# Linear attention and RWKV feed-forward on one core: a new order for the first tiles and the late weights

## The chip, the cores and the metric

The kernel runs on one core of a Trainium2 chip. The metric is the device time of one launch in microseconds (us). Engines are called TensorE (PE in the profile, with PEld for its weight loads), VectorE (DVE), ScalarE (ACT), GpSimd (POOL) and SyncE (SP, which issues most DMAs).

## The reference

The input `x` has 16 sequences of 1024 rows of 512 numbers, all in fp32. One layer is computed: linear attention with a residual and a layernorm, then an RWKV feed-forward with a residual and a layernorm.

```python
qkv = x @ Wqkv.T + bqkv
q, k, v = jnp.split(qkv, 3, axis=-1)
q = rmsnorm(q, gq); k = rmsnorm(k, gk)
q, k, v = split(q), split(k), split(v)            # 16 heads of 32
q = apply_rope(q, cos, sin); k = apply_rope(k, cos, sin)
qf = relu(q); kf = relu(k)
vpad = concatenate([v, ones])
vk = einsum('bhlp,bhld->bhpd', vpad, kf)          # per sequence and head
res = einsum('bhpd,bhld->bhlp', vk, qf)
attn = res[..., :-1] / (res[..., -1:] + 1e-6)
x = layernorm(x + rmsnorm(attn @ Wout.T + bout, gout))
# feed-forward: xr, xk mix each row with the row before it
r = sigmoid(xr @ W_r.T); k = square(relu(xk @ W_k.T))
x = layernorm(x + r * (k @ W_v.T))
```

## The kernel before

The 16384 rows are cut into 128 tiles of 128 rows. Phase A (the first half of the span) goes once over all tiles in slots, one tile `i` in each (`slot(i)`), eight tiles to a sequence. Phase B then makes the attention's output and the feed-forward in steps of 512 rows. This case is about the beginning of phase A.

A product of fp32 data is made as three products of float32r data: each operand is split into a high part (a cast on ScalarE) and a low part (the rest, a subtraction on VectorE or GpSimd), and high x high, high x low and low x high are summed in one PSUM bank. So q of a tile takes 12 matmuls of 128x128 by 128x512: four chunks of the 512 inputs times three (`proj(i, 0)`; `proj(i, 1)` is k). The bias comes in one of two ways: for tiles 0 and 1 by two more matmuls against a row that holds it (`row_h`, `row_l` with `sel_b`), for the later ones by a seed, a copy of the bias into the PSUM bank before the products (`seed`, in the profile a ScalarE COPY psq<-b_qk on line 157).

In a slot, TensorE makes q and k of tile `i` from the transposed input (`xt`, split by `split_x`), and adds the 12 products of the tile before into the keys' sum of the sequence, `pskx`, four banks (`add_kx(i - 1)`, from keys `kh`, `kl` and the untransposed input `xnh`, `xnl`). `rope` takes q and k from PSUM: the sum of squares (ScalarE, tile `junk`), two multiplications with tables and an addition (VectorE, tiles `t`, `ro`); q goes to DRAM (`q_d`); for the keys GpSimd makes the scale `rstd_all` and ScalarE the scaled, rectified `kh` and `ro`; GpSimd adds `ro` into `acc`.

The rotation needs four tables for each position in a sequence, two for q and two for k, with the gains `gqk` multiplied in. They are made once, for tiles 0 to 7 (`tables(i)`), and stored to DRAM (`tab_d`), from which the later tiles load them. The cosine table is a multiplication on GpSimd. The sine table, whose signs and places differ, is one matmul of `cs` and `gt` for each of q and k, which ScalarE copies out of PSUM; before, its bank is one of the `pskx` banks for tiles 0 and 1 (`psb`) and a bank of its own for tiles 2 to 7 (`pstab`). Each table has one SBUF buffer.

The q and k weights are loaded in eight blocks of 256 KB (`stage_qk`) and split (`split_qk`). Ten matmuls on zeros (`pswarm`) stand ahead of the first product. The 20 blocks of the other weights (v, out, and the three of the feed-forward) are late weights: from slot 5 on one block is loaded and split in each slot (`late_weight`, which calls `split_w`).

The order: an instruction stream is written down in Python and a scheduler with its own estimates orders each engine's stream, except where `in_order(engine)` holds the written order. Before, it holds for all five engines up to the end of the prologue (`start`), and for TensorE up to slot 7 (`start_pe`). Every engine works through its stream in order. DMAs take eight completion semaphores in turn, so that a DMA waits for the landing of the eighth before it.

The prologue before, in the written order of TensorE: warm-up, q of tile 0, `psb` products for `gt` and `cs`, q of tile 1, the sine tables of tile 0, k of tile 0, k of tile 1. Then slot by slot: (for tiles from 2) q, k, the key products of the tile before, the two sine tables of the next tile.

Of the kernel before, what the change touches and what calls it, by code (L numbers as in the profile page):

```python
# [24 lines left out]
NWARM = 10  # L25
# [8 lines left out]
def kernel(  # L34
# [259 lines left out]
    with ExitStack() as a_ctx:  # L294
# [44 lines left out]
        def split_w(hi, lo, src, low, dma, tag="xw", bufs=3):  # L339
            w = tp.tile([P, DIM], F32, tag=tag, bufs=bufs, name="wstage")  # L340
            dma.dma_start(out=w, in_=src)
            S.copy(hi, w)
            low.tensor_sub(lo, w, f32(hi))

        first = {}

        def seed(i):
            for j in range(2):
                first[i, j] = seeded(f"ps{'qk'[j]}{i}", b_qk[:, j * DIM : (j + 1) * DIM])
# [9 lines left out]
        def tables(i):  # L359

            t = i % 8
            if i < 8:
                tab_d[t] = dram.tile([P, 2, 2, DIM], F32, name=f"tab_d{t}")
            for j in range(2):
                for n in (1, 0):
                    tb = wa.tile([P, DIM], F32, tag=f"tab{j}{n}", name=f"tab{j}{n}{i}")
                    tab[i, j, n] = tb
                    if i >= 8:
                        nc.sync.dma_start(out=tb, in_=tab_d[t][:, j, n, :])
                        continue  # L370
                    g = g_qk[:, j * DIM : (j + 1) * DIM]
                    if n == 0:
                        c = angle[0][:, t, :].unsqueeze(1).to_broadcast([P, 2 * HEADS, HH])
                        G.tensor_mul(rows(tb), rows(g), c)
                    else:
                        ps = kx_bank(j) if i < 2 else bank(f"pstab{i}{j}")
                        T.matmul(ps, lhsT=cs[0:KT, t, :], rhs=gt[0:KT, j, :], start=True, stop=True)
                        S.copy(tb, ps)
                    nc.sync.dma_start(out=tab_d[t][:, j, n, :], in_=tb)
# [18 lines left out]

        mask = te.tile([P, P], BF16, name="mask")
        V.memset(mask, 0.0)  # L400
        for h in range(P // DH):
            V.memset(mask[h * DH : (h + 1) * DH, h * DH : (h + 1) * DH], 1.0)
        ones = te.tile([P, P], F32R, name="ones")
        V.memset(f32(ones), 1.0)
# [3 lines left out]
        def proj(i, j):  # L408

            seeds = i > 1  # L410
            ps = first.pop((i, j)) if seeds else bank(f"ps{'qk'[j]}{i}")
            cols = slice(j * DIM, (j + 1) * DIM)
            for c in range(NC_):
                for n, (a, b) in enumerate(((xh, "h"), (xh, "l"), (xl, "h"))):
                    T.matmul(  # L415
                        ps,
                        lhsT=a[i][:, c, :],
                        rhs=w_qk[b][:, c, cols],
                        start=(not seeds and c == 0 and n == 0),
                        stop=(seeds and c == NC_ - 1 and n == 2),  # L420
                        skip_group_check=True,
                    )
            if not seeds:
                for n, r in enumerate((row_h, row_l)):
                    T.matmul(
                        ps,
                        lhsT=sel_b[:, j, :],
                        rhs=r,
                        start=False,
                        stop=(n == 1),  # L430
                        skip_group_check=True,
                    )
            return ps

        acc, ros = {}, {}

        def rope(i, ps):

            ss = wa.tile([P, 2], F32, tag="ss", bufs=3, name=f"ss{i}")
            ro = []  # L440
            for j in range(2):
                S.activation(junk(f"{i}{j}"), ps[j], AF.Square, accum_out=ss[:, j : j + 1])
                r = wa.tile([P, DIM], F32, tag=f"ro{j}", bufs=1 + j, name=f"ro{j}{i}")
                t2 = wa.tile([P, DIM], F32, tag="t2", name=f"t2{j}{i}")
                V.tensor_mul(t2, ps[j], tab.pop((i, j, 1)))
                V.tensor_mul(ps[j], ps[j], tab.pop((i, j, 0)))
                V.tensor_add(halves(r), halves(ps[j]), halves(t2)[:, :, ::-1, :])
                ro.append(r)
                if j == 0:
                    q_d[i] = dram.tile([P, DIM], F32, name=f"q_d{i}")  # L450
                    nc.sync.dma_start(out=q_d[i], in_=r)
            V.tensor_scalar(ss, ss, 1.0 / DIM, RMS_EPS, ALU.mult, ALU.add)  # L452
            rsqrt(rstd_all[:, i, :], ss)
            k = ro[1]
            kh = tk.tile([P, DIM], F32R, tag="kh", bufs=2, name=f"kh{i}")
            kl = tk.tile([P, DIM], F32R, tag="kl", bufs=2, name=f"kl{i}")
            S.activation(kh, k, AF.Relu, scale=rstd_all[:, i, 1:2])
            S.activation(k, k, AF.Relu, scale=rstd_all[:, i, 1:2])  # L458
            V.tensor_sub(kl, k, f32(kh))
            b, t = divmod(i, 8)  # L460
            ros[i] = k
            if t == 1:
                acc[b] = tx.tile([P, DIM], F32, tag="acc", name=f"acc{b}")
                G.tensor_add(acc[b], ros[i - 1], k)
            if t > 1:
                G.tensor_add(acc[b], acc[b], k)  # L466
            return kh, kl
# [114 lines left out]
        def late_weight():  # L582
            n, w, c = late.pop(0)
            if n in "ao":
                to = {"a": w_a, "o": w_o}[n]
                split_w(to["h"][:, c, :], to["l"][:, c, :], w[:, c, :], V, nc.sync)
                return
            m = te.tile([P, 2, DIM], F32R, tag="m", bufs=2, name=f"w{n}{c}")
            split_w(m[:, 0, :], m[:, 1, :], w[:, c, :], V, nc.sync)
            nc.sync.dma_start(out=w_d[n][:, c, :, :], in_=f32(m))  # L590
# [7 lines left out]
        start_pe.enter_context(in_order(mybir.EngineType.PE))  # L598
        start = a_ctx.enter_context(ExitStack())
        for e in ("SP", "Activation", "DVE", "Pool"):  # L600
            start.enter_context(in_order(getattr(mybir.EngineType, e)))

        row = tp.tile([P, DIM], F32, tag="q", bufs=3, name="row")
        V.memset(row, 0.0)
        m0 = te.tile([P, 2, DIM], F32R, tag="m", bufs=2, name="m0")
        V.memset(f32(m0[:, 0, :]), 0.0)


        for n in range(NWARM):
            T.matmul(bank(f"pswarm{n}"), lhsT=m0[:, 0, 0:P], rhs=m0[:, 0, :], start=True, stop=True)  # L610
        stage = {}

        def stage_qk(j, c, dma=nc.sync):
            n = NC_ * j + c
            w = tp.tile([P, DIM], F32, name="wstage", **[dict(tag="x", bufs=NT), dict(tag="xw", bufs=3), dict(tag="q", bufs=3)][(n >= NT) + (n >= NT + 3)])
            dma.dma_start(out=w, in_=wqkv[:, c, j * DIM : (j + 1) * DIM])
            stage[j, c] = w

        def split_qk(j, c, low=V):
# [4 lines left out]
            low.tensor_sub(l, w, f32(h))  # L624

        load_xt(0)
        for c in range(NC_):
            stage_qk(0, c, (nc.sync, nc.scalar)[c % 2])
# [5 lines left out]

        S.copy(table, mhalf)
        angle = [tp.tile([P, 8, HH], F32, tag="y", bufs=2, name=f"angle{n}") for n in range(2)]
        nc.sync.dma_start(out=angle[1], in_=sin_t)
        stage_qk(1, 0)
        load_xt(1)
        for c in range(1, NC_):  # L640
            stage_qk(1, c)
        load_xn(0)
        nc.sync.dma_start(out=angle[0], in_=cos_t)
        g_qk = wp.tile([P, 2 * DIM], F32, tag="m", bufs=NC_, name="g_qk")
        nc.sync.dma_start(out=g_qk, in_=gqk.partition_broadcast(P))
        b_qk = ca.tile([P, 2 * DIM], F32, name="b_qk")
# [20 lines left out]
        V.tensor_scalar(msk[:, 1, :], msk[:, 0, :], -1.0, None, ALU.mult)  # L667
        cs6 = wp.tile([P, 8, P], F32, tag="m", bufs=NC_, name="cs6")[:, :, 0:KT]
# [5 lines left out]
        split_qk(0, 0)  # L674
        split_qk(0, 1)
# [4 lines left out]
        split_qk(0, 2)  # L680
        split_qk(0, 3)
        ahead = {(0, 0): proj(0, 0)}
        split_x(1)
        split_qk(1, 0, G)
        split_qk(1, 1, G)
        gt = wp.tile([P, 2, DIM], F32R, tag="m", bufs=NC_, name="gt")
        for j in range(2):
# [8 lines left out]
            )  # L696
        cs = wp.tile([P, 8, P], F32R, tag="m", bufs=NC_, name="cs")
# [16 lines left out]
        split_qk(1, 2, G)  # L714
        split_qk(1, 3, G)
        ahead[1, 0] = proj(1, 0)
        tables(0)
        ahead[0, 1] = proj(0, 1)
        split_xn(0)
        ahead[1, 1] = proj(1, 1)  # L720
        start.close()

        def slot(i):
# [6 lines left out]
            qk = [ahead.pop((i, j)) if i < 2 else proj(i, j) for j in range(2)]  # L730
            if 0 < i < N - 1:
                split_x(i + 1)
            if i > 0:
                split_xn(i)
# [8 lines left out]
            if i >= 1:  # L743
                add_kx(i - 1)
            state[i] = rope(i, qk)
            if not last:
                tables(i + 1)
                if i > 0:
                    seed(i + 1)
            if i == 2:  # L750
                with tc.issue_after(load.ins):
                    constants()
            if i >= 5 and late:
                with tc.issue_after(load.ins):
                    late_weight()
# [26 lines left out]
        for i in range(N - 1):  # L782
            slot(i)
            if i == 7:
                start_pe.close()
# [281 lines left out]
```

## Time and profile before

| | |
|---|---|
| time, median of 4 runs | 2729.34 us (2726.69 to 2729.4) |
| profiled execution | 2729.34 us, span 2727.5 us |
| TensorE busy | 2694.1 us (99%) |
| VectorE, ScalarE, GpSimd busy | 2170.1 (80%), 1882.2 (69%), 700.9 (26%) us |
| DMA | 433.29 MB, mean 159 GB/s |

A timeline line gives the start in the span, the duration, the engine, the line of the program and the operation; in square brackets stands how long the engine was idle before it, and what ended that. A line of waits gives who waited, for what, the sum in us, how often, and the longest. A line of stretches gives from:to, length, the busy time with the number of instructions for each engine asked for, the granted clock of TensorE, the share of the DMA engines' time and GB/s. TensorE's durations overlap: in full flow a product of 512 columns starts each 0.227 us and is listed with 0.39 us. The granted clock is listed as 1.00 at the start of the span too, where the products step by 0.43 us.

### The profile page before, as it was taken

The page shows a single profiled execution, that of the slowest core. Times are in us where ns is not written, and L with a number is a line of the kernel's source. Part 1 is how long each engine was busy: PE and PEld are TensorE (multiplying, and loading weights), DVE is VectorE, ACT ScalarE, POOL GpSimd, SP SyncE. Part 2 cuts the span into 40 slices and gives each one's busy share as a digit, 9 for nine tenths or more (in the row PEclk, how much of TensorE's full clock was granted, in tenths as well). Part 3 has the DMA queues.
Part 4 walks back from the last instruction along what each step waited for, and adds up shares of the span by engine and source line. Part 5 has one row for each costly group of instructions (what it writes and reads, how often), then busy time and mean ns, then how long its engine had stood idle before and what let it go on. Part 6 is the DMA issues. An engine that isn't in the chain of part 4 may idle for free.

```text
span 2727.5 us, 40197 instructions
## 1 busy us (share of the span) xinstructions
PE 2694.1 (99%) x12558; PEld 2233.1 (82%) x12558; DVE 2170.1 (80%) x4880; ACT 1882.2 (69%) x3822; POOL 700.9 (26%) x800
## 2 busy tenths in 40 slices
PE   8999999999999999999999999999999999999998
PEld 6778888888888888887888888888888888888887
DVE  6888787887787788776888878888887878888874
ACT  5666666666666656657777787777777777777775
POOL 5222222222222222223322222222222222222221
PEclk9999999999999999999999999999999999999999
DMA  6699777766777877764332232323233233313210
GB/s 231 205 307 317 234 247 232 231 227 225 230 232 248 263 246 245 233 205 157 101 105 74 93 109 64 111 89 110 65 95 110 73 98 93 116 59 108 75 56 34
DMA packets 232015, 433.29 MB, mean 159 GB/s; under 512 B 24676, under 2 KB 24932, under 8 KB 231800
## 3 DMA queue, kind: packets, MB, share of 16 engines
q1 hardware_dynamic: 231504, 430.18, 48.8%
q8 instruction: 99, 1.62, 0.2%
q14 instruction: 116, 0.95, 0.1%
q10 hardware_dynamic: 296, 0.53, 0.1%
HBM read 314.19 MB, written 116.42 MB: 158 GB/s over the span
## 4 chain that ended last, share of the span: by engine, by line
PE 84%; DVE 2%; DMA 2%; ACT 1%; issue 1%; POOL 0%; SPq 0%; POOLq 0%; DVEq 0%; ACTq 0%
PE psr L178 13%; PE psk L178 13%; PE psv L178 13%; PE psy L178 13%; PE psq L415 9%; PE pskx L485 9%; PE psk L415 9%; PE psqt L163 2%; PE pst L163 2%; PE psm L570 1%; PE pskv L528 1%; DMA q<-q_d 0%; DMA tab<-tab_d 0%; DMA q_d<-ro 0%; PE pskv L536 0%
## 5 line engine op out<-in xcount | busy, mean ns | idle before, releaser
L178 PE MATMUL psk<-mkh,w_k 128*128 128x512 f32 x1024 | 333.8, 397 | 2.3 <-ACT mkh L831 2.3
L178 PE MATMUL psv<-w_v,kah 128*128 128x512 f32 x1024 | 321.9, 395 | 0.0
L178 PE MATMUL psy<-mb,qth 128*128 128x512 f32 x1024 | 319.9, 389 | 0.0
L178 PE MATMUL psr<-w_r,mrh 128*128 128x512 f32 x1024 | 317.8, 396 | 0.0
L466 POOL TENSOR_TENSOR acc<-acc,ro 128x512 f32<-128x512 f32 x96 | 159.0, 1656 | 273.2 <-ACT ro L458 230.4
L178 PEld LDWEIGHTS psk<-mkh,w_k 128*128 128x128 f32 x1024 | 192.0, 189 | 41.6 <-ACT mkh L831 2.7
L178 PEld LDWEIGHTS psy<-mb,qth 128*128 128x128 f32 x1024 | 192.2, 188 | 39.9
L178 PEld LDWEIGHTS psr<-w_r,mrh 128*128 128x128 f32 x1024 | 188.8, 188 | 36.9
L178 PEld LDWEIGHTS psv<-w_v,kah 128*128 128x128 f32 x1024 | 187.8, 188 | 36.2
L142 POOL TENSOR_TENSOR rstd_all<-ss,mhalf 128x2 f32<-128x2 f32 x128 | 93.0, 726 | 475.4 <-DVE ss L452 453.9
L833 POOL TENSOR_TENSOR mkl<-mixk,mkh 128x512 fp32r<-128x512 f32 x127 | 165.8, 1306 | 184.3 <-ACT mkh L831 183.4
L415 PE MATMUL psq<-wqk_h,xh 128*128 128x512 f32 x512 | 201.8, 394 | 5.8 <-ACT psq L157 4.9
L415 PE MATMUL psk<-wqk_h,xh 128*128 128x512 f32 x512 | 199.6, 390 | 3.0 <-ACT psk L157 3.0
L415 PE MATMUL psq<-wqk_l,xh 128*128 128x512 f32 x512 | 200.8, 392 | 0.6 <-DVE wqk_l L624 0.6
L178 PE MATMUL psk<-mkl,w_k 128*128 128x512 f32 x512 | 200.5, 392 | 0.2 <-DVE mkl L833 0.2
L415 PE MATMUL psq<-wqk_h,xl 128*128 128x512 f32 x512 | 200.5, 392 | 0.0
L178 PE MATMUL psv<-w_v,kal 128*128 128x512 f32 x512 | 200.0, 391 | 0.0
L178 PE MATMUL psy<-mb,qtl 128*128 128x512 f32 x512 | 199.5, 390 | 0.0
L415 PE MATMUL psk<-wqk_h,xl 128*128 128x512 f32 x512 | 199.3, 389 | 0.0
L415 PE MATMUL psk<-wqk_l,xh 128*128 128x512 f32 x512 | 199.3, 389 | 0.0
L178 PE MATMUL psr<-w_r,mrl 128*128 128x512 f32 x512 | 196.1, 394 | 0.0
L142 POOL TENSOR_TENSOR yrs<-yss,mhalf 128x1 f32<-128x1 f32 x128 | 70.8, 553 | 404.6 <-DVE yss L286 295.3
(189 smaller groups left out, 7161.9 us busy)
## 6 DMA issues: line engine op xcount, KB each, us to landing
tab<-tab_d SPq DMA_DIRECT2D x480, 256.0 KB, 4.3
xt<-in_xt_dram SPq DMA_DIRECT2D x128, 256.0 KB, 4.6
xn<-in_x_dram SPq DMA_DIRECT2D x128, 256.0 KB, 4.4
q_d<-ro SPq DMA_DIRECT2D x128, 256.0 KB, 3.8
m_d<-m SPq DMA_DIRECT2D x64, 512.0 KB, 6.4
mb<-m_d SPq DMA_DIRECT2D x64, 512.0 KB, 6.3
q<-q_d SPq DMA_DIRECT2D x128, 256.0 KB, 2.9
out_dram<-x SPq DMA_DIRECT2D x128, 256.0 KB, 2.0
```

The lines of the kernel that those rows point to most:

```text
L142: G.tensor_tensor(dst, src, mhalf[:, 0 : src.shape[1]], ALU.pow)
L163: T.matmul(ps[:, n * P : (n + 1) * P], lhsT=b, rhs=ident, is_transpose=True, start=(n == 0), stop=(n == NC_ - 1), skip_group_check=True,)
L178: T.matmul(ps, lhsT=a[u][:, rows], rhs=b[w][:, cols], start=(afresh and c == 0 and k == 0), stop=(c == n - 1 and k == 2), skip_group_check ...
L415: T.matmul(ps, lhsT=a[i][:, c, :], rhs=w_qk[b][:, c, cols], start=(not seeds and c == 0 and n == 0), stop=(seeds and c == NC_ - 1 and n == 2),
L466: G.tensor_add(acc[b], acc[b], k)
L485: T.matmul(ps_kx[b][c], lhsT=a[:, c * P : (c + 1) * P], rhs=r, start=(t == 0 and n == 0), stop=(t == 7 and n == 2),)
L528: T.matmul(ps, lhsT=w_a["h"][:, c, cols], rhs=kx[:, c, g, :, :].rearrange("p two n -> p (two n)"), start=(g % 2 == 0 and c == 0), stop=Fal ...
L570: T.matmul(ps, lhsT=a[:, g, :], rhs=w_o[r][:, g, :], start=(n == 0), stop=(n == 2))
L833: (V if by_v else G).tensor_sub(ml, m, f32(mh))
```

## The change

- *Prologue.* The four blocks of q's weights, two of which went through ScalarE's DMA queue, all go through SyncE's. ScalarE loads its function table first of all. The zeros for the warm-up are set before the bias row; eight warm-up matmuls instead of ten. q of tile 0 (and k of tile 0) is made by parts: four matmuls high x high, four with the input's low part, four with the weights' low part, in place of the three of each chunk together. The high parts of a group of weight blocks are all cast before the low parts are made, and all low parts are VectorE's (`split_qk` gave those of k to GpSimd). The loads of x and tables are reordered; the masks are set later.
- *Order of the first eight tiles.* `early(i)` takes the place of `slot(i)` for tiles 0 to 7. In it q of the next tile is made before the key products of the tile before, and k of a tile in its own turn: k(i), sine table k of i+1, q(i+1), key products of i-1, sine table q of i+2. GpSimd too keeps the written order through these tiles. The sum of keys is a function of its own (`add_keys`). Tile 2 gets its bias by matmuls, like tiles 0 and 1.
- *Sine tables.* `rope_table(i, j)` makes the tables of q or k alone. For tiles 3 to 7 the sine product goes into the bank that the tile's q or k will use; once ScalarE has copied it out, the seed is copied over it. For tile 2 it goes into the `pskx` banks 2 and 3.
- *Late weights.* `late_load` loads a block in a slot, and `late_split` in the next slot writes its conversion.

```diff
-NWARM = 10
+NWARM = 8
...
-        def seed(i):
-            for j in range(2):
-                first[i, j] = seeded(f"ps{'qk'[j]}{i}", b_qk[:, j * DIM : (j + 1) * DIM])
+        def seed(i, j):
+            b = b_qk[:, j * DIM : (j + 1) * DIM]
+            if (i, j) in first:
+                S.copy(first[i, j], b)
+            else:
+                first[i, j] = seeded(f"ps{'qk'[j]}{i}", b)
...
-                        ps = kx_bank(j) if i < 2 else bank(f"pstab{i}{j}")
-                        T.matmul(ps, lhsT=cs[0:KT, t, :], rhs=gt[0:KT, j, :], start=True, stop=True)
-                        S.copy(tb, ps)
+                    ps = kx_bank(j + 2 * (i == 2)) if i < 3 else bank(f"ps{'qk'[j]}{i}")
+                    T.matmul(ps, lhsT=cs[0:KT, t, :], rhs=gt[0:KT, j, :], start=True, stop=True)
+                    S.copy(tb, ps)
+                    if i > 2:
+                        first[i, j] = ps
...
-            seeds = i > 1
+            seeds = i > 2
...
+            three = ((xh, "h"), (xh, "l"), (xl, "h"))
+            order = [(p, c) for c in range(NC_) for p in three]
+            if by_part:
+                order = [(three[n], c) for n in (0, 2, 1) for c in range(NC_)]
...
-        def late_weight():
+        def late_load():
             n, w, c = late.pop(0)
+            st = tp.tile([P, DIM], F32, tag="xw", bufs=3, name="wstage")
+            nc.sync.dma_start(out=st, in_=w[:, c, :])
+            staged.append((n, c, st))
+
+        def late_split():
+            n, c, st = staged.pop(0)
...
+            S.copy(h, st)
+            V.tensor_sub(l, st, f32(h))
...
-            stage_qk(0, c, (nc.sync, nc.scalar)[c % 2])
+            stage_qk(0, c)
...
-        ahead = {(0, 0): proj(0, 0)}
+        ahead = {(0, 0): proj(0, 0, by_part=True)}
...
-        split_qk(1, 2, G)
-        split_qk(1, 3, G)
+        lows = [split_qk(1, c) for c in (2, 3)]
+        for low in lows:
+            low()
         ahead[1, 0] = proj(1, 0)
-        tables(0)
-        ahead[0, 1] = proj(0, 1)
+        rope_table(0, 0)
+        rope_table(0, 1)
         split_xn(0)
-        ahead[1, 1] = proj(1, 1)
         start.close()
+
+        def early(i):
+
+            load = load_xt(i + 2)
+            rope(i, 0, ahead.pop((i, 0)))
+            rope_table(i + 1, 0)
+            if i > 1:
+                seed(i + 1, 0)
+            rope(i, 1, proj(i, 1, by_part=(i == 0)))
+            rope_table(i + 1, 1)
+            if i > 1:
+                seed(i + 1, 1)
+            if i > 0:
+                split_x(i + 1)
+                split_xn(i)
+                ahead[i + 1, 0] = proj(i + 1, 0)
+                add_kx(i - 1)
+            load_xn(i + 1)
+            add_keys(i)
+            if i == 2:
+                with tc.issue_after(load.ins):
+                    constants()
+            late_step(i, load)
+
+        def late_step(i, load):
+            if staged:
+                late_split()
+            if i >= 5 and late:
+                with tc.issue_after(load.ins):
+                    late_load()
...
-        for i in range(N - 1):
+        for i in range(8):
+            early(i)
+        start_pe.close()
+        for i in range(8, N - 1):
             slot(i)
-            if i == 7:
-                start_pe.close()
```

## The prediction

> **What bounds the kernel now.** I read the page first, then TensorE's busy time by stretch, then who TensorE waits for, then timelines of the stretches with waits.
>
> ```profile
> span 2727.5 us, 40197 instructions
> ...
> PE 84%; DVE 2%; DMA 2%; ACT 1%; issue 1%; POOL 0%; SPq 0%; POOLq 0%; DVEq 0%; ACTq 0%
> ```
>
> TensorE is the bound. Its busy time by stretch (length, PE busy, count, granted clock, DMA share, GB/s):
>
> ```profile
> 0.00:34.00 34.00, 27.58 (x97) 1.00 0.70 228
> 34.00:100.00 66.00, 62.03 (x267) 1.00 0.66 224
> 100.00:200.00 100.00, 93.20 (x431) 0.98 0.82 272
> 200.00:1200.00 1000.00, 998.03 (x4617) 1.00 0.76 243
> ```
>
> It idles 6.4 us to 34, 4.0 to 100, 6.8 to 200, and 2.0 in the next 1000. The edit touches tiles up to about 25 (250 us); so some 17 us of idle time, plus slow-clock time, is all there is to win. The waits of TensorE, first 0 to 34 us, then 34 to 300:
>
> ```profile
> PE pskx L485 <- ACT tab L378: 2.5, 1, 2.5
> PE psq L415 <- ACT wqk_h L623: 0.9, 1, 0.9
> PE psq L415 <- DVE wqk_l L624: 0.6, 1, 0.6
> ...
> PE psq L415 <- ACT psq L157: 4.9, 3, 2.8
> PE psk L415 <- ACT psk L157: 3.0, 3, 1.4
> PE pskx L485 <- DVE kx L500: 2.2, 1, 2.2
> PE pskx L485 <- ACT kh L457: 0.7, 1, 0.7
> ```
>
> The timelines behind them (start, duration, what):
>
> ```profile
> 2.23 4.63 PE L610 MATMUL pswarm<-m 128*128 128x512 f32 x10 [2.23 <-DVE m L606]
> 4.68 0.49 ACTq L630 DMA_DIRECT2D row<-in_gqk_dram  x1
> 5.20 1.28 ACT L635 ACT_TABLE_LOAD   x1 [5.20 <-DMA xt<-in_xt_dram]
> 7.11 1.13 ACT L623 CAST wqk_h<-wstage 128x512 fp32r<-128x512 f32 x2
> 10.17 0.63 PE L415 MATMUL psq<-wqk_h,xh 128*128 128x512 f32 x1
> 10.60 0.63 PE L415 MATMUL psq<-wqk_l,xh 128*128 128x512 f32 x1
> 14.79 0.39 PE L690 MATMUL psb<-row_h,sel_g 128*128 128x512 f32 x1
> 36.89 0.59 ACT L378 COPY tab<-pstab 128x512 f32<-128x512 f32 x1 [2.15 <-DMA tab_d<-tab]
> 106.11 0.62 ACT L342 CAST wout_h<-wstage 128x512 fp32r<-128x512 f32 x1 [3.98 <-DMA wstage<-in_wout_dram]
> 185.09 1.44 PE L485 MATMUL pskx<-kh,xnh 128*128 128x512 f32 x3 [2.16 <-DVE kx L500]
> ```
>
> ScalarE's table load stands behind its own DMA issues, the last of which waits for x, so the first weight is split only at 7.11 and q of tile 0 starts at 7.78. Its products step by 0.43 us; from 14.79 on the step is 0.227. Later ScalarE waits for a table's store (36.89) and for a late weight (106.11), and the seeds behind them reach TensorE late. After the wait at 185.09 eight products step by 0.43 again.
>
> **The change, part by part.** *First q.* ScalarE now begins with the table load: 0.75 + 1.28 + 0.19 = 2.2; its two row DMAs (1.07 + 0.49) end at 3.8. The first x landed by 4.68 beside a second queue; alone I take 3.9, x's high part 4.5, first weight's 5.1, first product 5.2. The five 0.262 MB blocks now share one queue. Two rows price it:
>
> ```profile
> 4.20:5.40 1.20, 1.20 (x5) 0.91 (x4) 0.00 (x0) 0.20 (x1) 0.00 (x0) 1.00 1.06 408
> 7.50:9.90 2.40, 1.54 (x3) 0.94 (x4) 2.40 (x4) 2.40 (x6) 0.45 (x1) 1.00 0.90 294
> ```
>
> The first stretch has two queues at work (408 GB/s), the second one (294). Bytes move from about 2.0, so the last block lands at 2.0 + 1.31 MB / 294 = 6.5, its high part is there at 7.1, the fourth product starts at 7.2. By parts, the order is four high, four with x's low, four with the low weights, two bias products: ten steps of 0.43 after the fourth, so the next stage starts at 11.9 instead of 14.79: gain 2.9. At 408 GB/s ScalarE's 0.52 per split binds and it is 3.4; at 228 (the mean of 0 to 34) 1.7. The Trainium skill, DMA: Bandwidth & Descriptors, Issuing engines are not separate DMA queues, says that all queues run on the same 16 engines, so that a second saves only issue time; by it one queue also carries 408 and the gain is 3.4; the two rows above differ, so I keep 294.
>
> Two warm-up products fewer cost nothing: eight take 7 x 0.43 + 0.79 = 3.8 us, from 1.4 (their zeros are now set first: 0.86 + 0.48) to 5.2, where q begins. The step stayed at 0.43 through 4.63 us of warm-up here and fell only at 14.7; I assume that it stays until q0 ends, with 2.0 us more gain if it falls right after the fourth product (ten steps of 0.2 less) and 1.7 less if it falls 8 steps later. The skill, TensorE: Matmul & The Clock Gate, Part 1, counts in free-running windows of 3.4 us that must be busy, which speaks against a shorter warm-up; by it eight hardly fill one window, and the release would come about 3.4 to 6.8 us after 7.2, inside these bounds.
>
> *Tables of tiles 0 and 1.* From 11.9 everything to q1's end repeats 14.79 to 19.76 (4.97): 16.9. VectorE now makes all low parts that GpSimd made (3.40 + 2.54 for four): gt 1.29, two low parts 1.28, cs 1.29 from 12.9 give 16.8, against 16.9; but low parts run at up to 1.76 each beside GpSimd, so the first table may wait 0 to 1.3: take 0.2. The third sine product writes a bank that ScalarE must first copy (0.58 and some 0.2, less one product): lose 0.6. k0 then ends at 21.5.
>
> *q a tile ahead.* Between 26.62 and 33.37, 6.75 us, TensorE does 14 products (3.2): 3.5 is lost to tile 0's keys. Now q2 (3.2 us) stands ahead of them. Next late is kh0: on ScalarE it comes after the square of k1 (k1 ends near 25.1), so at about 27.1; the keys' product comes at 28.5. All 3.5 gained.
>
> *Sine tables in their tile's bank.* The wait for k2's seed (36.35 to 38.15, less 0.23: 1.6) goes; the seed of q(i+1) now needs its own table's product, copy and seed: 0.23 + 0.58 + 0.58 + 0.2 = 1.6 of latency, under k(i)'s twelve products (2.7) and one more. For q3 a store landing late leaves 0.2. Tile 2 gets four bias products: 4 x 0.227 = 0.9 lost. The three waits at tiles 5 to 8 (0.9, 0.8, 0.7, each some 0.2 more from start to start: 3.0) are of this kind; I keep 0.5 of them: gain 2.5. GpSimd in written order: table 1.3, table 1.3, rstd 0.7, sum 1.8 = 5.1 of a slot of 8.65 us: hidden; with that cover gone each 1 us over is 1 us a tile.
>
> *Late weights.* The wait of 2.8 at 107.7, behind the 3.98 on ScalarE, mostly goes, since the conversion now stands after q10's seed; next late is the copy of kx, 0.8: gain 2.0. The wait of 2.2 before 185.09 goes with the 8 x 0.2 = 1.6 of slow steps after it, because the built order puts q18 between: 3.8, keep 3.3. Of the other two (1.2, 0.7) 0.6. New waits in a changed order, -0.9. Sum 5.0, bounds -1 to 8.5. From about tile 26 each engine has the same order as before.
>
> Sum: 2.9 - 0.2 - 0.6 + 3.5 + 1.6 - 0.2 - 0.9 + 2.5 + 5.0 = 13.6. The profiled execution took 2729.34 (span 2727.5 and 1.8 around it), which is also the median; I predict 2716.
>
> **The rivals.** *Everything goes:* the clock falls into place at q0's fourth product (2.0) and no wait stays up to tile 18 (0.5 + 0.2 + 3.5): 2709. For it: the new order has 1.3 us of cover on every seed. Against: VectorE is busy 89% of 60 to 80, so something will be late.
>
> *The late part doesn't do what it says:* in the built order the first conversion of a late weight still stands between the two uses of tile 3's keys on ScalarE, as before; if the others keep waiting for their DMA too, the 5.0 is nought and half of the 2.5 goes: 13.6 - 6.3 = 7.3, 2722. For it: four waits of 9.2 us in all on the wout blocks. Against: q10's seed has passed its conversion.
>
> *Little at all:* the one queue runs at 228, the tables' first waits are at their bound (1.3), and waits return elsewhere: 13.6 - 1.2 - 1.1 - 6.3 - 2 = 3, 2726.
>
> *Slower: stores hold the tables.* Each sine table has one buffer, so its copy waits until the store of the tile before has landed, and ScalarE with it, now ahead of the seeds of q as well. Price: the row at 36.89, 2.15 on ScalarE, 1.4 on TensorE. There are 14 such copies in tiles 1 to 7; without the 2.5 the gain is 11.1, so from 12 blocked copies (16.8) on it is slower by over 5.5; all 14 give 2729.3 - 11.1 + 19.6 = 2738. Against: stores land in 3.0 us (4.3 at most to 100 us), and copies of one table are 8.65 apart.
>
> **How the numbers follow.** Forecast 0.60 (2712 to 2720 by itself), everything 0.12, late part 0.16, little 0.07, slower 0.05. Faster by over 0.2% (5.5 us, about what a measurement of this kernel can tell from no change) means below 2723.9: the first three less 0.03 for the late part's upper end, 0.85; within 0.2%: 0.10; slower 0.05. The range reaches down to the first rival and up past the second: 2708.5 to 2723.5.
>
> **What would show it.** After: the first psq product near 5.2 and the first psb product near 11.9; no wait of pskx on a table copy, one short wait of psb (0.6); the key products of tile 1 done near 40 with q3 behind them, instead of 43.7 without it; no wait of psq over 1 us between 60 and 200, and no slow steps near 180. Wrong if ScalarE's copies wait for stores in most early tiles, if the first q still ends past 14, or if the late weights' waits stand in front of seeds as before.

## The result, and the profile after

The changed kernel takes 2732.22 us (median of 33 runs, 2726.47 to 2736.69), the kernel before 2728.45 in the runs beside it (median of 53): 1.0014 times as long, 95% interval 1.0009 to 1.0018. It is 3.8 us slower by these medians; the two profiled executions, 2727.5 and 2733.0 us in span, lie 5.5 apart. Forecast was 13.3 faster, 2716.

The page and TensorE's stretches of the changed kernel, in the columns of before:

```profile
span 2733.0 us, 40181 instructions
...
PE 86%; DMA 1%; DVE 1%; ACT 1%; issue 0%; POOL 0%; SPq 0%; POOLq 0%; DVEq 0%; ACTq 0%
```

```profile
0.00:34.00 34.00, 27.91 (x100) 1.00 0.78 249
34.00:100.00 66.00, 61.55 (x255) 0.95 0.66 218
100.00:200.00 100.00, 97.04 (x452) 1.00 0.81 265
200.00:1200.00 1000.00, 991.44 (x4582) 1.00 0.76 242
```

Against the same stretches of the kernel before, the first line gains three products, the third 21. The second loses twelve and has a granted clock of 0.95, the last loses 35. So time is won at the start and from 100 to 200 us, and lost from 34 to 100 and after 200. TensorE's waits to 34 us, then from 34 to 300:

```profile
PE pskx L484 <- ACT tab L375: 2.9, 1, 2.9
...
PE psq L411 <- ACT wqk_h L638: 1.3, 1, 1.3
PE psb L374 <- ACT tab L375: 0.4, 1, 0.4
...
PE psq L411 <- ACT psq L344: 4.5, 2, 3.1
PE pskx L484 <- DVE kx L499: 3.1, 2, 2.9
...
PE psq L411 <- ACT psq L157: 1.4, 1, 1.4
```

The waits for seeds of line 157 (4.9 and 3.0 before) are mostly gone; 1.4 is left. In their place stand a wait of the key products for a table copy (one of 2.5 us before, 2.9 now, and now with q2 already behind it), two waits on seeds that lie in a table's bank (line 344), and one for a key bank. The timeline rows behind them:

```profile
5.06 0.63 PE L411 MATMUL psq<-wqk_h,xh 128*128 128x512 f32 x1
6.27 1.95 ACT L638 CAST wqk_h<-wstage 128x512 fp32r<-128x512 f32 x3 [1.49 <-DMA wstage<-in_wqkv_dram]
13.13 0.47 PE L707 MATMUL psb<-row_h,sel_g 128*128 128x512 f32 x1
32.36 0.17 DVE L389 TENSOR_SCALAR omm_k<-mu_k 128x4 f32<-128x4 f32 x1 [0.75 <-DMA mu_k<-in_mu_k_dram]
33.16 0.59 ACT L375 COPY tab<-psb 128x512 f32<-128x512 f32 x1 [2.23 <-DVE t L440]
33.79 0.79 PE L484 MATMUL pskx<-kh,xnh 128*128 128x512 f32 x1 [2.92 <-ACT tab L375]
77.44 0.62 ACT L597 CAST wa_h<-wstage 128x512 fp32r<-128x512 f32 x1 [2.92 <-DMA wstage<-in_wqkv_dram]
80.73 0.50 PE L411 MATMUL psq<-wqk_h,xh 128*128 128x512 f32 x1 [3.10 <-ACT psq L344]
260.83 0.47 PE L484 MATMUL pskx<-kh,xnh 128*128 128x512 f32 x1 [2.92 <-DVE kx L499]
```

Rows 4 to 6 are one chain: VectorE's next step, `t` of k1, stands behind a small operation that waits for its load; that step reads the only buffer of k's sine table; the copy of tile 2's table into this buffer waits for it; and the copy's source is key bank 3, which the fourth key product of tile 0 needs. Rows 7 and 8 are the other: a late weight's conversion waits for its load, the copies for q7 stand behind it, and TensorE waits for the seed (the expectation of e2 below calls the two tiles 5 and 6; they are 6 and 7). Row 9 is the first key product of tile 24: in the built order two of these stand ahead of the products of q26, where the kernel before has q26 first (from 259.08), and they wait for VectorE's copy out of the key bank. After each of the two long stalls up to 100 us (2.92 and 3.10 us) some eight products step by 0.43 us again, 1.6 us each.

To compare whole kernels I add up, from the trace, what the time between the starts of two products has over the 0.228 us of full flow, where that is over 0.12 (stalls and slow steps). It is one profiled execution of each kernel, so a difference of a few tenths says nothing; the ratio is that of the repeated runs, with its interval. Columns are us of the span:

| kernel | 0-30 | 30-100 | 100-200 | 200-320 | 320-1200 | ratio to before |
|---|---|---|---|---|---|---|
| before | 9.8 | 5.4 | 9.1 | 0.8 | 1.6 | 1 |
| after | 7.3 | 11.0 | 4.0 | 6.1 | 3.5 | 1.0014 (1.0009-1.0018) |
| e1 | 10.1 | 11.1 | 2.8 | 4.6 | 3.8 | 1.0008 (0.9999-1.0017) |
| e2 | 6.6 | 5.1 | 3.9 | 5.9 | 1.9 | 0.9996 (0.9987-1.0004) |
| e3 | 7.9 | 4.4 | 5.6 | 6.1 | 1.9 | 0.9980 (0.9972-0.9989) |
| e4 | 8.4 | 4.0 | 5.7 | 7.6 | 2.7 | 1.0014 (1.0005-1.0023) |
| e5 | 7.2 | 3.6 | 3.6 | 4.0 | 1.2 | 0.9981 (0.9972-0.9990) |
| e6 | 8.6 | 3.0 | 5.4 | 4.8 | 0.8 | 0.9973 (0.9963-0.9984) |
| e7 | 7.0 | 2.7 | 3.2 | 5.7 | 0.7 | 0.9970 (0.9958-0.9981) |
| e8 | 5.8 | 10.8 | 3.7 | 6.5 | 4.6 | 1.0006 (0.9997-1.0015) |
| e9 | 7.3 | 3.5 | 3.2 | 4.0 | 1.6 | 0.9980 (0.9971-0.9989) |
| e10 | 7.8 | 2.3 | 1.3 | 5.0 | 1.4 | 0.9966 (0.9954-0.9977) |
| e11 | 7.5 | 2.5 | 4.5 | 4.0 | 3.0 | 0.9968 (0.9955-0.9980) |
| e12 | 8.8 | 4.9 | 4.6 | 3.5 | 1.2 | 0.9994 (0.9985-1.0002) |
| e13 | 6.9 | 3.0 | 0.0 | 5.5 | 2.1 | 0.9960 (0.9947-0.9974) |
| e14 | 7.9 | 11.4 | 2.6 | 4.0 | 4.5 | 1.0015 (1.0006-1.0024) |
| e15 | 7.8 | 5.3 | 0.0 | 3.1 | 0.6 | 0.9956 (0.9944-0.9969) |

The largest wait of the last column is one for the low part of a tile's keys near 910 us (1.27 us before, 2.31 in the changed kernel); no experiment deals with it.

### The profile page after: what moved, and what is told of

It reads as the page before. It is cut to its first block, busy times and chain, and to the rows that moved or that the text cites. A ratio compares the mean times of both kernels' runs of the same rounds, so it can differ in the third digit from the quotient of the medians.

```text
span 2733.0 us, 40181 instructions
## 1 busy us (share of the span) xinstructions
PE 2696.8 (99%) x12560; PEld 2234.0 (82%) x12560; DVE 2173.1 (80%) x4884; ACT 1882.0 (69%) x3820; POOL 691.4 (25%) x796
## 4 chain that ended last, share of the span: by engine, by line
PE 86%; DMA 1%; DVE 1%; ACT 1%; issue 0%; POOL 0%; SPq 0%; POOLq 0%; DVEq 0%; ACTq 0%
PE psr L178 13%; PE psv L178 13%; PE psy L178 13%; PE psk L178 13%; PE psq L411 9%; PE pskx L484 9%; PE psk L411 9%; PE psqt L163 2%; PE pst L163 2%; PE psm L569 1%; PE pskv L527 1%; DMA tab<-tab_d 1%; PE pskv L535 0%; DMA q_d<-ro 0%; DMA q<-q_d 0%
```

## The experiments

**e1: tile 2's tables out of the key banks.**

```diff
-ps = kx_bank(j + 2 * (i == 2)) if i < 3 else bank(f"ps{'qk'[j]}{i}")
+ps = kx_bank(j) if i < 2 else bank(f"ps{'qk'[j]}{i}")
...
-seeds = i > 2
+seeds = i > 1
```

> The sine tables of tile 2 go into the banks of that tile's own q and k, as those of tiles 3 to 7 do, and are seeded by a copy; the four bias products of tile 2 go. Theory (the key bank is what held the key products of tile 0): the wait of 2.92 us of the fourth pskx product at 33.8 us and the half-clock spell after it (8 products 0.2 us longer, 1.6) are gone, and four products of 0.23 (0.9) with them: 5.4 us off, 2727 against 2732, and the end of the key products of tile 0 some 4.5 us earlier. Rival (the wait only moves): ScalarE's copies are late in any order, q2's seed or the keys of tile 0 are waited for instead, and less than 2 us comes of it: 2730 to 2732.

Measured 2730.88 against 2728.43 of the kernel before beside it. The key products wait no more, but q2 does:

```profile
29.87 0.80 PE L411 MATMUL psq<-wqk_h,xh 128*128 128x512 f32 x1 [2.52 <-ACT psq L344]
```

On ScalarE the square of k1, both keys of tile 0 and q2's table copy stand ahead of that seed. The rival holds: the wait moved.

**e2: the conversion can't be pulled ahead.** For tiles 6 to 8:

```diff
+if i <= PIN:                               # PIN = 8
+    with tc.issue_after(xn_copy[i].ins):   # ScalarE's cast of xn
+        late_split()
...
```

> The conversions of the late weights in the slots of tiles 6 to 8 are tied behind ScalarE's conversion of the natural-order rows of the same tile, so that the scheduler can't pull them ahead of it. Theory (the conversion waits for its load in front of ScalarE's queue): the waits of 2.10 and 2.92 us of that conversion at 65.8 and 77.4 us go, and with them the 1.36 and 3.10 us of TensorE on the seeds of q5 and q6 and the half-clock spell at 81.5 (1.6): 6.1 off, 2726. Rival (the conversion only pushes other copies later, or the load itself is what delays): a seed or a key is waited for nearby, gain under 2, 2730 to 2732.

Measured 2726.47, 5.8 us under the changed kernel, as the theory has it. Only the conversions of four blocks and their low parts change their place, and from 34 to 100 us no wait of TensorE is left but the one at 34 us:

```profile
PE pskx L487 <- ACT tab L378: 3.4, 1, 3.4
```

This cause is shown: a conversion that waits for its load stood in front of the seeds.

**e3: both.**

> Both of the former. If the two stalls are separate and nothing downstream takes the time back: 5.4 + 6.1 = 11.5 off, 2721 (7 to 8 under the kernel before). If time won before 100 us is given back later (the rival: VectorE's work per tile or the loads set the pace there), 2726 to 2729, with new waits between 100 and 310 us.

Measured 2721.95. The profiled execution (2727.19, the longest of its eleven) has q2's wait of 2.5 us as in e1, and no wait of TensorE from 34 to 100 us. Nearly the forecast sum came, though e1 alone had given little; the intervals of e1 and e2 are as wide as that difference.

**e5: only k's table of tile 2 out of the key bank.** On top of e2; q2 keeps its bias products.

```diff
+ps = kx_bank(j + 2 * (i == 2)) if i < 2 + (j == 0) else bank(f"ps{'qk'[j]}{i}")
...
+seeds = i > 2 - j
```

> e2 with the tables of tile 2 divided: q's stays in the key bank (q2 keeps its bias products and waits for no seed), k's goes into the bank of k2, which is seeded. Two bias products go. Theory (the key products of tile 0 wait for the copy of k's table alone, q2 for its seed alone): both the wait of 3.4 us of pskx at 34 us (e2) and that of 2.5 us of psq at 30 us (e3) are gone, with one half-clock spell of 1.6; against e2 (2726.5) 4 to 5 us less, 2722, and the end of the key products of tile 0 at 33 us where e2 had 36.2. Rival (ScalarE and VectorE are late with the keys themselves): the key products then wait 2 us or more for kh, xnl or kl of tile 0, and it stays at 2725 to 2727.

Measured 2724.37. The trace shows the theory: no wait at the key products of tile 0, which end 3.6 us earlier than in e2; k2's seed is late by 1.1 and q3's by 0.7.

```profile
30.11 1.07 PE L487 MATMUL pskx<-kh,xnh 128*128 128x512 f32 x4
...
34.30 0.50 PE L414 MATMUL psk<-wqk_h,xh 128*128 128x512 f32 x1 [1.07 <-ACT psk L347]
```

Of the 4 to 5 us, 2.1 are seen in the medians.

**e7: the small operations on mu later.** On top of e6, below.

```diff
-V.tensor_scalar(omm[n], mu[n], -1.0, 1.0, ALU.mult, ALU.add)
...
+if i == 4:
+    with tc.issue_after(xn_low[i].ins):    # VectorE's xnl of tile 4
+        for n in "kr":
+            V.tensor_scalar(omm[n], mu[n], -1.0, 1.0, ALU.mult, ALU.add)
```

> e6 with the two small operations on mu put behind VectorE's xnl of tile 4 instead of ahead of k1's rotation, where they waited for their loads (0.75 us in the changed kernel, 2.03 and 0.52 in e3). Theory (VectorE's chain of tile 1 is late by that wait and passes it on): the keys of tile 1 and the tables of tile 3 come 1 to 2 us earlier, and 0.5 to 2 us come off TensorE's waits before 60 us. Rival (VectorE has room there): TensorE's waits are those of e6, same time.

Measured 2721.83 against e6's 2721.58. In e6 VectorE waited 2.07 and 1.56 us there; without it TensorE's waits for the seeds of k2 and q3 are 1.0 and 0.3 instead of 1.3 and 1.3. About 1 us in the trace, nothing that the medians resolve.

**e8: q's weights on two queues again.**

```diff
-stage_qk(0, c)
+stage_qk(0, c, (nc.sync, nc.scalar)[c % 2])
```

> The changed kernel with q's four weight blocks on two queues in turn, as before. Theory (one queue brings the second block late): the second high product, which waited 1.66, 0.84, 2.49 and 1.50 us in four runs of the one-queue beginning, waits 0.5 us or less, the four high products end near 7.5 instead of 8.5 us, and the first block comes no later; the whole is 0.5 to 1.5 us less, 2731. Rival (it is the engines that the queues share, with the rows of tiles 0 and 1, that set the arrival): the products start at the same times within 0.5 us, the time is the same.

Measured 2731.10. Bytes from 4.0 to 6.2 us (stretch, length, ScalarE busy, clock, DMA share, GB/s), first the changed kernel, then e8:

```profile
4.00:6.20 2.20, 0.78 (x2) 1.00 0.88 273
```

```profile
4.00:6.20 2.20, 1.75 (x3) 1.00 1.05 388
```

The two queues carry 388 GB/s where one carried 273 (313 in e1, 250 in e2; 399 before, with two). The fourth high product starts at 7.62, 0.65 us earlier than in the changed kernel; the first starts 0.5 later, which the theory had not. So the second block does come earlier with two queues, but it is worth about 1 us, no more than the runs can tell. A ceiling of one queue is not shown: in the changed kernel SyncE's queue alone carries 414 GB/s from 2.5 to 3.0 us and 385 from 8 to 9, and the low mean comes from stretches like 4.5 to 5.0 us, with 115 GB/s while blocks issued by 3.0 had not landed.

**e4: the late weights' part alone, in the kernel before.** `late_weight` is divided into `late_load` in one slot and `late_split` in the next.

> The kernel before with only the late weights changed: loaded in one slot, converted in the next. The prediction's step (the conversion then finds its load there) gives 5 us off, 2723. The rival that the trace after suggests (the scheduler pulls the conversion to the same place on ScalarE as before, so it still waits): within 2 us of before, 2726 to 2730, with ScalarE's conversions again waiting 2 to 3 us for wstage between 100 and 200 us.

Measured 2731.42 against 2728.43: 3 us *slower*, outside both. ScalarE's waits for `wstage` are 8.6 us in sum, 11.3 before: for the first eight blocks the scheduler put the conversion in the place it had before. From the ninth block on the conversions did go back by about a tile, to 234.3 to 251.8 us for the last four, and there are 7.6 us of stalls from 200 to 320 us, though none beside these four: 2.1 at 217 and 227 us, 1.6 at 257, 3.9 at 297 and 302.

**e12: e4, begun one tile earlier** (`if i >= 4 and late`), so that the conversions stand where they were and only the loads are earlier.

> e4 (the kernel before with loads and conversions of the late weights a slot apart) begun one tile earlier: the conversions stand where the kernel before has them, and only the loads are a slot earlier. Theory A of e9: the stalls between 100 and 200 us stay at e4's 5.7 (before 9.1), those between 200 and 320 us go from e4's 7.6 back to 1 to 2, so 5 us off e4: 2726. Theory B: 200 to 320 us stays above 4, and the time near 2730.

Theories A and B are those of e9, below. Measured 2726.17, 5.2 under e4. The last four conversions now run from 224.7 to 241.8; stalls from 200 to 320 us fall from 7.6 to 3.5, not to 1 or 2. Theory A has the size of the gain. Its mechanism is not shown: the stalls that went stood at 217, 257 and 297 to 302 us, not beside the last conversions. In this stretch e12 still has 2.7 us more than the kernel before.

**e14: the new beginning alone**, with the late weights loaded and converted in one slot.

> The changed kernel with the late weights loaded and converted in one slot as before: the new beginning alone. If the two parts add up, as e4 (late weights alone) cost 3.0 us and both together 3.8, it costs 0.8: 2729, with stalls of 11 us between 30 and 100 us as in the changed kernel, 7 to 9 between 100 and 200 us and 1 to 2 between 200 and 320 us. If the loss after 200 us belongs to the beginning too (TensorE early), 200 to 320 us keeps 4 us or more and the time is 2731 or above.

Measured 2731.12 against 2726.14. The two parts don't add up: each alone costs as much as both (1.0014 and 1.0015, both 1.0014). The waits on table seeds are there without any division of the late weights:

```profile
PE psq L411 <- ACT psq L344: 4.9, 2, 2.9
```

So it is the new beginning that makes TensorE need the seed of q(i+1) a tile sooner, and the conversion, where it always stood (66.9 and 78.4 us here, 67.4 and 76.8 before), is now in the way. And from 100 to 200 us this kernel has 2.6 us of stalls with the late weights as before, against 9.1. TensorE comes there later and loses less: the last key product of tile 6 starts at 96.8 against 92.7 before, that of tile 8 at 113.6 against 113.3.

**e6: q26 ahead of the key products of tile 24.** On top of e5:

```diff
+if i == 25:
+    seed(i + 1, 0)
+    ahead[i + 1, 0] = proj(i + 1, 0)
+    with tc.issue_after(last_mm[0].ins):   # behind q26's last product
+        add_kx(i - 1)
...
```

> e5 with TensorE's order held in one place: the twelve products of q26 before the first key products of tile 24, as in the kernel before (the scheduler puts two key products ahead of them in every kernel with the new beginning). Nothing else moves on any engine. Theory (time won before 100 us is given back at 255 us by that order): the wait of 2.7 to 3.4 us on the key banks goes, 3 us off e5. Rival (the wait moves to the next step, kl of tile 28 or q26's seed): under 1 us off.

Measured 2721.58 against e5's 2724.37, the 3 us of the theory, though the two intervals overlap. In the trace it is rather the rival: the wait of 2.7 us for the key banks becomes one of 2.1 for q26's seed. Which of the two holds stays open. That the order belongs to every kernel with the new beginning was wrong: e14 has q26 ahead by itself.

**e9: the late weights as before from tile 9 on**, on top of e7.

> e7 with the late weights converted in the slot of their load from tile 9 on, as in the kernel before. Counted by TensorE's stalls and slow products in a stretch: 100 to 200 us had 9.1 us before and 3.2 in e7, 200 to 320 us had 0.8 before and 5.7 in e7. Theory A (a tile later, the conversions of the last weights fall beside the end of the third sequence and its rotations, on the same two engines): 200 to 320 us goes down to 1 to 2, 100 to 200 us goes up to 6 to 8, and the time stays near 2722. Theory B (TensorE, come earlier, runs up against ScalarE's and VectorE's work of these tiles, wherever the conversions stand): 200 to 320 us stays at 4 to 6.

Measured 2723.57. From 200 to 320 us 4.0 instead of 5.7, from 100 to 200 us 3.2 as in e7. Neither theory: A's loss between 100 and 200 us did not come, B's lower end fits the rest.

**e11: e7, begun one tile earlier** (`if i >= 4 and late`).

> e7 with the late weights begun one tile earlier (load from tile 4, conversion from tile 5), so that the last conversions stand where they stood before. Theory A of e9: TensorE's stalls between 200 and 320 us go from 5.7 to 1 to 2 while those of 100 to 200 us stay near 3, 3 to 4 us off e7: 2718. Theory B: 200 to 320 us stays at 4 to 6, 2722.

Measured 2718.57: the time of theory A, but with 4.0 us of stalls left from 200 to 320 us, which is theory B's (in a profiled execution of 2723.29, near the longest of its six).

**e10: every conversion tied behind its tile's rows** (`PIN = 30` instead of 8), on top of e7.

> e7 with every late conversion, not only those of tiles 6 to 8, tied behind the conversion of the natural-order rows of its tile. Theory (a conversion that can't be pulled ahead of its load never stops ScalarE): ScalarE's waits for wstage, 6 us in all in e2, are under 1, and 1 to 3 us come off TensorE's stalls between 100 and 200 us: 2720. Rival (the order of everything else is set anew by the scheduler, and the conversions now stand in front of keys and seeds): stalls of the same size elsewhere, 2721 to 2724.

Measured 2719.14. ScalarE waits for `wstage` nowhere any more, and the stalls from 100 to 200 us fall from 3.2 to 1.3.

**e13 and e15: e10 begun at tile 4, and at tile 2.**

> e10 and e11 together: every late conversion tied behind its tile's natural-order rows, and the series begun one tile earlier. If both gains are real and separate, 1 to 3 us less than either (2719.1, 2718.6): 2717, with stalls of 1 to 2 us between 100 and 200 us and 4 or less between 200 and 320 us. Rival (the stalls after 200 us are TensorE come early, whatever stands beside it): 200 to 320 us stays at 4 to 5 and the time at 2719.

> e13 with the series begun at tile 2, so that the last conversion stands two tiles before the place it has in the kernel before. Theory A (conversions beside the end of the third sequence): nothing of them is left there, 200 to 320 us has under 2 us of stalls, and the time is 2 us under e13. Theory B (TensorE early): 200 to 320 us stays at 3.5 to 5; the conversions beside tiles 3 to 5 may cost up to 2 us more before 100 us.

Measured 2717.44 and 2715.73 against 2726.14. e13 has the time of its first theory and, with 5.5 us from 200 to 320 us, the stalls of its rival; e15's 3.1 there is neither theory's. TensorE no longer waits between 100 and 200 us; e15 in the stretches 100 to 200 and 200 to 320:

```profile
100.00:200.00 100.00, 100.00 (x474) 1.00 0.85 282
200.00:320.00 120.00, 117.55 (x533) 1.00 0.85 282
```

From 200 to 320 us e15 keeps 3.1 us, with no late weight left beside the end of the third sequence: waits for two seeds of k (1.3) and for a low part of the keys (1.1). e15 beats both kernels: 0.9956 of before (0.9944 to 0.9969), and 0.9942 of after (0.9956 / 1.0014). It ends where the changed kernel was forecast to end, by changes that the forecast did not contain.

## Why the prediction was wrong, step by step

By stretches: to 100 us a gain of 8.6 was forecast; the stalls went from 15.2 to 18.3 and two products were added, 3.6 lost. From 100 to 320 us a gain of 5.0; the stalls went from 9.9 to 10.1. After 320 us another 1.9 was lost, where nothing was forecast. Together that is 19.3, about the forecast gain of 13.6 and the 5.5 by which the profiled executions differ; by the medians the miss is 17.4.

- *First q.* The first product was right (5.06 for 5.2). The end was 13.13 for 11.9: the second block came at 6.2, and the four high products started at 5.06, 6.94, 7.6 and 8.27, the last 1.1 later than forecast. Gain 1.66 instead of 2.9. And the base was one execution: with the beginning of before the first psb product comes at 14.79 (before), 12.49 (e4) and 13.20 (e12), with the new one and one queue at 11.54 to 13.24 in 13 executions. By the means, 13.49 and 12.62, the step is worth about 0.9, and the term was mis-sized by 2. The 294 GB/s taken for one queue came out near the mean of 4.0 to 6.2 us (273, against 388 in e8), but as a rate of one queue it was wrong: this queue alone carried 414 and 385 GB/s in other stretches of the same execution. The Trainium skill, DMA: Bandwidth & Descriptors, Issuing engines are not separate DMA queues, has a second queue save only the issue time. These rows don't contradict that as a limit; why the second block still came later on one queue is open.
- *Tables of tiles 0 and 1.* Right: one wait of 0.4 us for a table copy.
- *q a tile ahead: "Next late is kh0 ... All 3.5 gained."* This step failed first. kh0 came at 27.45 (forecast 27.1), but a key product needs its bank too, and banks 2 and 3 held tile 2's sine products, as the diff says. I followed the operand and not the output. My own view of before names the bank, too: `PE pskx L485 <- ACT tab L378: 2.5`. There kh0 was done at 29.24 and the product started at 29.76, when the copy out of its bank was done. In the changed kernel the 3.5 us became a wait of 2.92 and 1.6 us at half clock. e1 moved the wait to q2's seed; in e5 it is gone, with 1.1 and 0.7 left at two later seeds.
- *Sine tables in their tile's bank: "I keep 0.5 of them: gain 2.5."* I set the latency of a seed against the products that cover it, and left out what else stands on ScalarE ahead of the seed. The conversion of a late weight does, and it waits 2.10 and 2.92 us for its load. The three waits of 3.0 us became 1.36 and 3.10, with 1.6 of slow clock. e2 shows it whole: 5.8 us. The second rival had seen the conversion's place, and had priced it only as a gain that stays out.
- *Late weights, 5.0.* e4 measures this term by itself: 3 us lost. In the changed kernel it is worth nothing (1.0014 with it, 1.0015 without, e14), and what is won there between 100 and 200 us comes with the new beginning alone. The scheduler, not the slot in which a line is written, places a conversion that is not tied; so the first eight waited for their loads as before. The later blocks did move back by a tile, and loading and converting them a tile earlier takes 5.2 us off e4 (e12); how their place costs that is open.
- *"From about tile 26 each engine has the same order as before"* is not so: in the traces TensorE's order is that of the kernel before only from 326 us on. And 200 to 320 us went from 0.8 to 6.1 us of stalls. Up to there the losses of the first 100 us had been made up: the last key product of tile 23 starts at 254.57 and at 254.32 before. For tile 24, with two of its products ahead of q26, it is 267.41 against 264.29.
- *The rivals.* None was right. The one that foresaw a slower kernel named the stores of the tables; no copy waited for a store in the place that decided.

Open: the 3 to 6 us that stay between 200 and 320 us in all mended kernels. e15 shows that conversions beside them are not needed for it. That TensorE comes there 8 to 13 us earlier than before (the start of tile 23's last key product: 254.32 before, 246.71 to 241.32 in e5, e7, e10, e13 and e15) and meets ScalarE's and VectorE's own work there would fit these five. It can't be the whole: the changed kernel, e1, e8 and e14 come to the same product at 254.0 to 255.2, as late as the kernel before, and have 4.0 to 6.5 us of stalls there. No run here isolates it.

## What to carry to other kernels

A product waits for its operands and for its output bank: when work is moved ahead, ask of the bank who held it last and what that holder waits for. When a consumer is moved a tile ahead, list everything that stands before its producer on the producer's engine, above all operations that wait for a DMA, and tie those behind it. And a gain near the start is not always kept: of the 13.0 us by which e13 is ahead of the kernel before at the key products of tile 23, 10.4 are left at tile 33; of e7's 8.9, 6.6.

## What the runs showed of the hardware

- The granted clock changes in steps of about 3.41 us: the half-clock spells in the traces last 3.41 or 6.83 us. With one and the same beginning it rose first at 4.5 to 6.1 us of the span in seven executions, where it fell back for 3.41 us after another 3.41, and at 10.4 to 13.6 us in six. Together with the arrival of the second weight block (second product at 6.11 to 7.57 us) this leaves the end of the first stage 1.7 us apart in these executions (11.54 to 13.24), more than the 0.9 that the change does there.
- A stall need not fill such a window to cost one. A wait of 2.16 us before 185 us in the kernel before, and one of 2.14 us before 40.34 us in e15, were each followed by 3.41 us at half clock; one of 2.92 us before 260.83 us in the changed kernel was not. The Trainium skill, TensorE: Matmul & The Clock Gate, Part 1, has windows of 3.4 us that run freely, whenever a kernel starts. The lengths of the spells agree. That a stall's place in the window decides would fit both cases; no run here separates it.
